# Four residual layers on 8x16x16 images: activations relaid from [sample, w] to [w, sample]

## The chip, the cores and the metric

The kernel runs on one core of one Trainium2 chip. The metric is the device time of one execution in microseconds, as the median of several runs.

## The reference

The input x is fp32, 8192 samples of 8 channels by 16 rows (h) by 16 columns (w). Four layers are applied one after the other, each on a group-normalized copy (4 groups of 2 channels, mean and variance over channel, h and w), with its result added to x:

```python
x = x + tt_matvec([core0, core1, core2], gn(x)) + bias0      # layer 0: tensor-train product, rank 8
x = x + relu(batchnorm(conv3x3(gn(x), w1) + b1))             # layer 1: statistics over all samples
x = x + conv3x3(quant(gn(x)), quant(w2)) / (sx * sw) + b2    # layer 2: sx = 127 / max|gn(x)| over all samples
x = x + conv3x3(edge_pad(gn(x)), sign(w3) * mean|w3|) + b3   # layer 3
```

Layers 1 and 2 each need one number over all samples, so the work falls into three stages.

## The kernel before

The samples are cut into 64 tiles of 128. A tile is a 128x2048 fp32 array: the partition is (channel, h), the free axis is (sample, w), w innermost. The helpers `samples(t)` and `over_w(stat, a, b)` view it as [128, sample, w] and spread a statistic per sample over w. A quarter is 32 samples, 512 columns.

Each engine executes its instructions in the order of the program, which is kept by the wrapper `InOrder`; therefore nearly all instructions carry the line of that wrapper, L43, and are told apart by the names of the tiles. A name before `<-` is the output, those behind it are inputs.

**Stage 1** (layer 0 and the convolution of layer 1) goes quarter by quarter, 256 of them. `limbs`, `fetch` and `expand` split the normalized x and multiply it by core2 (`pu<-core2r,xl`, copied to `u` by ACT). `main` multiplies `u` by the other cores: eight fp32 matmuls of 512 columns into the PSUM tile `po`, each recorded as two. DVE then adds `po` to x (`xs<-po,xs`). `norm_sums` and `norm_stats` (at steps r=1 and r=4 of `main` in each tile's first quarter, for the tile before) sum x and its square over w with `reduce_w` (`s<-xs`, `s<-sq`); `group_stats` finishes them and `norm_apply` writes the padded copy `x1n`. `conv1_scaled` (ACT) and `conv1_input` (POOL) form the inputs `v` of a fast convolution along w, `conv1` multiplies them (`pm`, `pc`), and `conv1_output` (DVE) combines them into `ys`, of which `bn_stats` follows. `po`, `pm` and `pc` come from one PSUM pool with three buffers, one of each per quarter:

```python
pe.matmul(samples(po)[:, a:b], core01[:, r], u[:, a:b, r, :], start=(r == 0), stop=(r == R - 1))
```

**Stage 2** finishes layer 1, takes the group statistics for layer 2 and the largest normalized value. Per tile: load x and y, ReLU with scale and offset (ACT), add (POOL), square (ACT), `sums_pe` (PE, `gs`), a reduction and a transpose on DVE (`s_c`, `psc`), the power on POOL, `to_rows` on DVE (`diag_b`, `rows_c`) and two matmuls (`gb`, `gr`) that spread the statistics, the centring of x (DVE) and the range, a reduction of |x| over w (`top`). The steps of tile i and of the tiles up to three before it alternate. Most tiles are stored (`x2_d`) and 13 stay in SBUF.

**Stage 3** does the convolution of layer 2 and layer 3. The order of its steps is a fixed list: `TURN`, repeated for each tile, with the head `C_HEAD` and the tail `C_TAIL` written out. Per tile: `rows2` and `spread2` give the scale per sample (`ps_a`); `v` multiplies it in and rounds to int8 (DVE); `q` makes bf16 of it (ACT); `c2h0` and `c2h1` are the convolution in two halves (`pq`, six bf16 matmuls each, four of the twelve per tile covering all 512 columns and eight of them 480); `stz` adds the first half to x (DVE); `z1` (ACT) and `add1` (POOL, `bs`) add the second; `sq`, `sums` (`s<-`), `small`, `pow`, `rows3` and `spread3` are the statistics for layer 3 (`ps_r`, `ps_o`); `t` scales (DVE), `hi` (ACT) and `lo` (POOL) split it in two fp32r parts with edge columns; `c` and `corr` add an offset per sample (ACT, POOL); `c3h0` and `c3h1` are the second convolution (`pf`, 24 fp32r matmuls of 512 columns); `out0` and `out1` add it to x (DVE). `pq` and `pf` rotate through two PSUM buffers.

Of the kernel before, what the change touches and what calls it, by code (L numbers as in the profile page):

```python
# [18 lines left out]
P = 128  # L19
# [3 lines left out]
G = 4  # L23
# [24 lines left out]
C_HEAD = """  # L48
rows2:0 spread2:0 v:0 rows2:1 q:0 spread2:1 c2h1:0 rows2:2 bias:0 v:1 spread2:2 rows2:3 c2h0:0 v:2 z1:0 q:1
spread2:3 stz:0 add1:0 bias:1 c2h1:1 sq:0 c2h0:1 z1:1 v:3 sums:0 stz:1 small:0 q:2 add1:1 c2h0:2 c2h1:2 bias:2  # L50
rows2:4 pow:0 sq:1 rows2:5 rows3:0 z1:2 spread2:4 spread3:0 stz:2 t:0 q:3 sums:1 hi:0 c:0 small:1 v:4 add1:2 pow:1
bias:3 c2h0:3 spread2:5 rows3:1 sq:2 c2h1:3 spread3:1 stz:3 lo:0 sums:2 t:1 rows2:6 corr:0 edl:0 small:2 c:1 q:4
z1:3 hi:1 c3h0:0 pow:2 c3h1:0 v:5 add1:3 rows3:2 out0:0 bias:4 out1:0 lo:1 sq:3 q:5 spread3:2 spread2:6 c2h0:4 c:2
corr:1 edl:1 c2h1:4 rows2:7 z1:4 stz:4 t:2 hi:2 sums:3 c3h1:1 small:3 v:6 c3h0:1 out1:1 c2h1:5 pow:3 bias:5 rows3:3
spread3:3 lo:2 out0:1 q:6 spread2:7 rows2:8 z1:5 edl:2 v:7 c:3 add1:4 sq:4 c2h0:5 c3h0:2 bias:6 t:3 corr:2 stz:5
sums:4 c3h1:2 small:4 add1:5 hi:3 out0:2 c2h0:6 pow:4 rows3:4 sq:5 out1:2 spread2:8 stz:6 spread3:4 t:4 lo:3 c2h1:6
z1:6 corr:3 edl:3 sums:5 c:4 hi:4 small:5 pow:5 bias:7 v:8 q:7 add1:6
""".split()
C_TAIL = """
c2h1:-4 sq:-5 rows2:-2 rows3:-6 out1:-8 spread3:-6 rows2:-1 spread2:-2 c2h0:-4 v:-2 sums:-5 stz:-4 z1:-4 q:-3 t:-6  # L60
edl:-7 c3h0:-7 q:-2 small:-5 c2h1:-3 c:-6 out0:-7 c2h0:-2 hi:-6 add1:-4 sq:-4 pow:-5 rows3:-5 z1:-3 spread3:-5
bias:-2 t:-5 stz:-2 lo:-6 edl:-6 sums:-4 small:-4 bias:-3 corr:-6 c:-5 spread2:-1 c2h0:-3 stz:-3 pow:-4 c3h1:-7
hi:-5 out1:-7 c3h0:-6 rows3:-4 spread3:-4 add1:-3 c2h1:-2 sq:-3 lo:-5 z1:-2 out0:-6 v:-1 c3h1:-6 edl:-5 q:-1 add1:-2
sums:-3 t:-4 corr:-5 c:-4 c3h1:-5 out1:-6 small:-3 sq:-2 pow:-3 hi:-4 out1:-5 lo:-4 rows3:-3 bias:-1 sums:-2 c2h1:-1
small:-2 z1:-1 spread3:-3 edl:-4 c2h0:-1 c3h0:-5 c:-3 t:-3 stz:-1 add1:-1 pow:-2 corr:-3 rows3:-2 c3h1:-4 hi:-3
spread3:-2 sq:-1 out0:-5 c:-2 corr:-4 sums:-1 t:-2 lo:-3 hi:-2 small:-1 pow:-1 out1:-4 c3h0:-4 corr:-2 rows3:-1
out0:-4 edl:-3 c3h0:-3 spread3:-1 t:-1 lo:-2 c3h1:-3 out0:-3 edl:-2 out1:-3 hi:-1 c:-1 lo:-1 c3h0:-2 c3h1:-2 edl:-1
out0:-2 c3h0:-1 out1:-2 corr:-1 c3h1:-1 out0:-1 out1:-1
""".split()

# [8 lines left out]
def tile_net(ctx: ExitStack, tc: tile.TileContext, xb, xt_in, pack0, pack1, pack2, out):  # L79
# [84 lines left out]
    def late_constants(late):  # L164
# [99 lines left out]
        mod32 = const.tile([P, 32], F32, name="mod32")  # L264
# [5 lines left out]
        for k, name in enumerate(("sel0", "sel1", "corr")):  # L270

            t = L[name] = const.tile([P, CH], F32, name=name)
            dve.tensor_copy(t.rearrange("p (g n) -> p g n", g=G),
                            mod32[:, G * k:G * k + G].unsqueeze(2).to_broadcast([P, G, CH // G]))
        yield "statistics"

    def diagonal(n):
        ts = []
        for k in range(2):
            t = const.tile([P, NQ, 32], F32, name=f"diag_{n}_{k}")  # L280
            nc.gpsimd.memset(t, 0.0)
            ts.append(t)
        return ts
# [6 lines left out]
    HALVES = [(0, P // 2), (P // 2, P)]  # L290

    def samples(t):
        return t.rearrange("p (b w) -> p b w", w=W)

    def over_w(stat, a, b):

        return stat[:, a:b].unsqueeze(2).to_broadcast([P, b - a, W])

    def reduce_w(dst, src, op=ALU.add):
        for a, b in HALVES:  # L300
            dve.tensor_reduce(dst[:, a:b], samples(src)[:, a:b], AX.X, op)
# [21 lines left out]
    with first as s:  # L323
# [13 lines left out]
        x1n = [const1.tile([P, P, W + 2], F32, name=f"x1n_{k}") for k in range(2)]  # L337
        for t in x1n:
            pool.memset(t[:, :, 0:W + 2:W + 1], 0.0)
# [13 lines left out]
        def add_bias(t):  # L353
            v = samples(T[t]["x"])
            pool.tensor_tensor(v, v, bias0_t.unsqueeze(1).to_broadcast([P, P, W]), ALU.add)
# [76 lines left out]
        def main(t, q, between, n0=None):  # L432
# [3 lines left out]
            for a, b in parts:  # L436
                for r in range(R):
                    for f, args in between.get(r, ()) if b == QS else ():
                        f(*args)
                    pe.matmul(samples(po)[:, a:b], core01[:, r], u[:, a:b, r, :], start=(r == 0), stop=(r == R - 1))  # L440
            cols = slice(q * BANK, (q + 1) * BANK)
            x = T[t]["x"]
            dve.tensor_tensor(x[:, cols], po, x[:, cols], ALU.add)
# [12 lines left out]
        def norm_apply(t):  # L456
            group_spread(spread1, T[t].pop("mv"), 32)
            x, xn = samples(T[t]["x"]), x1n[t % 2][:, :, 1:W + 1]
            for a, b in HALVES:
                for k, op, i in ((0, ALU.subtract, x), (1, ALU.mult, xn)):  # L460
                    dve.tensor_tensor(xn[:, a:b], i[:, a:b], over_w(spread1[:, k], a, b), op)


        def quarter_stats(t, q):
            cols, x = slice(q * BANK, (q + 1) * BANK), T[t]["x"]
            sums = small.tile([P, 2, QS], F32, name=f"sq_{t}_{q}", tag="sums")
            act.activation(xh[:, cols], x[:, cols], AF.Square)
            for k, src in enumerate((x, xh)):
                dve.tensor_reduce(sums[:, k], samples(src)[:, q * QS:(q + 1) * QS], AX.X, ALU.add)
# [3 lines left out]
        def quarter_apply(t, q):  # L473
            spread = spreads[q % 2]
            group_spread(spread, T[t].pop(("mv", q)), 32)
            b = slice(q * QS, (q + 1) * QS)
            x, xn = samples(T[t]["x"])[:, b], x1n[t % 2][:, b, 1:W + 1]
            for k, op, i in ((0, ALU.subtract, x), (1, ALU.mult, xn)):
                dve.tensor_tensor(xn, i, over_w(spread[:, k], 0, QS), op)
# [4 lines left out]
        def conv1_scaled(t, q):  # L484

            x = x1n[t % 2][:, q * QS:(q + 1) * QS]
            x4, x2 = (wk.tile([P, QS, n], F32, name=f"{k}_{t}_{q}", tag=k, bufs=1) for k, n in (("x4", W), ("x2", W // 2)))
            act.activation(x4, x[:, :, 0:W], AF.Copy, scale=4.0)
            act.activation(x2, x[:, :, 1:W:2], AF.Copy, scale=2.0)
            T[t]["x4", q] = x4, x2  # L490

        def conv1_input(t, q):
            x = x1n[t % 2][:, q * QS:(q + 1) * QS]
            x4, x2 = T[t].pop(("x4", q))
            e, r = (wk.tile([P, n, QS, W // 4], F32, name=f"{k}_{t}_{q}", tag=k, bufs=1) for k, n in (("e", 4), ("r", 2)))
            v = wk.tile([P, 6, QS, W // 4], F32, name=f"v_{t}_{q}", tag="v")
            pool.tensor_tensor(e.rearrange("p k b j -> p b j k"), *(t.rearrange("p b (j k) -> p b j k", k=4)
                                                                    for t in (x[:, :, 2:W + 2], x4)), ALU.subtract)
            pool.tensor_tensor(r[:, 0], x2[:, :, 1:W // 2:2], x2[:, :, 0:W // 2:2], ALU.subtract)
            pool.tensor_tensor(r[:, 1], x[:, :, 4:W + 1:4], x[:, :, 2:W:4], ALU.subtract)  # L500
            pool.tensor_tensor(v[:, 0], e[:, 2], e[:, 1], ALU.add)
            pool.tensor_tensor(v[:, 1], e[:, 2], e[:, 1], ALU.subtract)
            pool.tensor_tensor(v[:, 2], r[:, 1], r[:, 0], ALU.add)
            pool.tensor_tensor(v[:, 3], r[:, 1], r[:, 0], ALU.subtract)
            pool.tensor_tensor(v[:, 4:6], e[:, 2:4], e[:, 0:2], ALU.subtract)
            T[t]["v", q] = v.rearrange("p i b j -> p i (b j)")
# [14 lines left out]
        def conv1_direct(t, q):  # L521

            x = x1n[t % 2][:, q * QS:(q + 1) * QS]
            po = ps_m.tile([P, BANK], F32, name=f"pd_{t}_{q}", tag="mm")
            for k in range(3):
                pe.matmul(samples(po), L["band1"][:, k], x[:, :, k:k + W], start=(k == 0), stop=(k == 2))
            act.activation(T[t]["y"][:, q * BANK:(q + 1) * BANK], po, AF.Identity, bias=L["b1"], scale=1.0)
# [5 lines left out]
        def conv1_stats(t, q):  # L533
            dve.bn_stats(T[t]["bst"][:, q], T[t]["y"][:, q * BANK:(q + 1) * BANK])
# [6 lines left out]
        def conv1_output(t, q):  # L541
# [7 lines left out]
            s1, d3, d1, s3 = sd[:, 0], sd[:, 1], pm[:, 1], pm[:, 3]  # L549
            y = T[t]["y"][:, q * BANK:(q + 1) * BANK].rearrange("p (n k) -> p k n", k=4)  # L550
            ends = wk.tile([P, 2, NC], F32, name=f"ends_{t}_{q}", tag="ends", bufs=1)
            dve.tensor_tensor(ends[:, 0], s1, po[:, 0], ALU.add)
            dve.scalar_tensor_tensor(ends[:, 1], d3, 8.0, po[:, 1], ALU.mult, ALU.add)
# [154 lines left out]
    def sums_pe(ps, x, sq):  # L708

        for k, src in ((0, x), (1, sq)):  # L710
            for q in range(NQ):
                pe.matmul(ps[32 * q:32 * q + 32], L["wsum"][:, k], src[:, q * BANK:(q + 1) * BANK],
                          start=(k == 0), stop=(k == 1))


    def put_quarter(ps):
        nc.vector.tensor_copy(ps[:, 0:NQ], L["quarter"])

    def stats_small(mv, st, ps, name):

        s = small.tile([P, 32], F32, name=f"s_{name}", tag="s")
        dve.tensor_reduce(s, samples(ps), AX.X, ALU.add)
        dve.transpose(st, s)
# [399 lines left out]
```

## Time and profile before

| | us |
|---|---|
| median of 3 runs (lowest, highest) | 3833.41 (3831.76, 3834.64) |
| profiled execution, span from first to last instruction | 3831.5 |
| stage 1: first instruction to last product of layer 1's convolution | 0 to about 2620 |
| stage 2: to the end of the largest value | about 2620 to 3063 |
| stage 3: to the end | about 3063 to 3831 |
| stage 3, first output stored, last output stored (issue) | 3105.8, 3826.4 |

For the profiled execution only its span is listed; the three run times lie 0.3 to 3.1 above it. In the table of busy time by stretch a row gives the stretch, its length, and for each engine the busy microseconds with the number of instructions; then the TensorE clock that was granted (1.00 is full), the busy share of the DMA engines and the bytes per time. In the timeline a row gives the start, the length, the engine, the line, the operation, the tiles, the shape, the count and in brackets the idle time before it with what ended it. Matmul records overlap, so their spacing from start to start, and not their length, is what they cost on a full PE.

### The profile page before, as it was taken

Reading aid. Unit: us, or ns where it says so; the run is one execution under the profiler, and the core shown is the slowest. Engines: PE = TensorE matmul, PEld = TensorE weight load, DVE = VectorE, ACT = ScalarE, POOL = GpSimd, SP = SyncE. Lnnn points to the kernel's source line nnn. Section 1 sums busy time; section 2 is a strip of 40 time slices with the busy share of each in tenths; the row PEclk is TensorE's granted clock in tenths of the full one; section 3 lists DMA queues with packets and bytes.
Section 4 is the critical chain, followed back from the end, with each engine's and each line's share of the span. In section 5 each row is a group of like instructions: output and inputs, shape, how many; then the busy total and the mean of one; then the engine's idle time right before and its main releaser. Section 6 shows DMA issues by size and latency. Waiting matters only on the chain. (4 is left out here: it accounts for less than half of the span.)

```text
span 3831.5 us, 52833 instructions
## 1 busy us (share of the span) xinstructions
PE 3606.5 (94%) x16326; PEld 2127.6 (56%) x16326; DVE 3406.9 (89%) x6319; ACT 2513.1 (66%) x2673; POOL 3040.9 (79%) x3101
## 2 busy tenths in 40 slices
PE   8999999999999999999999999997655599999998
PEld 4666666666666666666666666662211155555555
DVE  8988888888888888888888888877998889999997
ACT  5666666666666666666666666665665477777775
POOL 4877778777777787777777877766887779999997
PEclk9999999999999999999999999998776699999999
DMA  5787787888877878788788788757999724444432
GB/s 212 255 268 258 258 266 251 270 253 262 270 256 258 267 250 271 253 262 267 258 261 266 250 271 252 258 187 281 422 425 425 301 110 176 187 185 178 185 145 99
DMA packets 210809, 960.93 MB, mean 251 GB/s; under 512 B 44896, under 2 KB 45152, under 8 KB 110048
## 3 DMA queue, kind: packets, MB, share of 16 engines
q1 hardware_dynamic: 173808, 692.22, 48.7%
q0 software_dynamic: 36288, 264.26, 23.4%
q8 instruction: 131, 2.15, 0.2%
q14 instruction: 150, 1.23, 0.1%
q10 hardware_dynamic: 432, 1.08, 0.1%
HBM read 578.84 MB, written 378.54 MB: 250 GB/s over the span
## 5 line engine op out<-in xcount | busy, mean ns | idle before, releaser
L43 PE MATMUL po<-u,core 128*128 128x512 f32 (+1 forms) x4112 | 1844.7, 591 | 0.0
L43 ACT COPY u<-pu 128x2048 f32<-128x2048 f32 x512 | 956.7, 1868 | 511.9 <-PE pu L43 511.8
L43 PEld LDWEIGHTS po<-u,core 128*128 128x128 f32 x4112 | 744.7, 190 | 737.1 <-issue 736.1
L43 PE MATMUL pu<-core2r,xl 128*128 128x256 f32 x4032 | 678.5, 310 | 4.5 <-ACT u L43 3.6
L43 PEld LDWEIGHTS pu<-core2r,xl 128*128 128x128 f32 x4032 | 527.9, 189 | 127.8 <-issue 123.0
L43 POOL TENSOR_TENSOR bs<-bs,xh 128x512 fp32r<-128x512 f32 (+1 forms) x253 | 325.6, 1287 | 201.0 <-ACT xh L43 200.9
L43 POOL TENSOR_TENSOR v<-e 128x128 f32<-128x128 f32 x750 | 397.9, 542 | 0.0
L43 DVE TENSOR_TENSOR xs<-po,xs 128x512 f32<-128x512 f32 x256 | 177.0, 692 | 217.5 <-PE po L43 217.5
L43 ACT ACTIVATE m<-pm,b 128x128 f32<-128x128 f32 x250 | 92.0, 368 | 395.5 <-PE pm L43 395.5
L43 PEld LDWEIGHTS pm<-v,fast 128*128 128x128 f32 x2000 | 262.5, 191 | 119.7 <-issue 106.2
L43 POOL TENSOR_TENSOR e<-x1n,x 128x512 f32<-128x512 f32 x250 | 306.2, 1225 | 23.9 <-ACT x L43 16.4
L43 DVE TENSOR_TENSOR bs<-bs,stat 128x1024 f32<-128x1024 f32 x252 | 290.8, 1217 | 2.1
L43 POOL TENSOR_TENSOR xs<-xs,w 128x2048 f32<-128x2048 f32 x64 | 291.5, 4554 | 0.6 <-DMA xs<-in_xt 0.6
L43 PE MATMUL pm<-v,fast 128*128 128x128 f32 x2000 | 263.6, 275 | 0.0
L43 ACT ACTIVATE x<-x1n 128x512 f32<-128x512 f32 x500 | 247.1, 545 | 7.6 <-DVE x1n L43 7.6
L43 POOL TENSOR_TENSOR mv<-mv,mhalf 128x4 f32<-128x4 f32 x127 | 130.8, 1030 | 138.1 <-DVE mv L43 138.1
L43 PE MATMUL pf<-hi,sign 128*128 128x512 f32 x768 | 227.7, 434 | 0.5 <-DVE xs L43 0.5
L43 POOL DMA_DIRECT2D xl<-limb_d x252 | 150.0, 595 | 96.9 <-ACT x L43 29.1
L43 PE MATMUL pf<-lo,sign 128*128 128x512 f32 x768 | 219.4, 423 | 0.0
L43 POOL TENSOR_TENSOR v<-r 128x128 f32<-128x128 f32 x500 | 215.9, 448 | 0.0
L43 ACT ACTIVATE sq<-xs 128x2048 f32<-128x2048 f32 x103 | 196.8, 1911 | 4.7 <-POOL xs L43 4.6
L43 PE MATMUL gb<-rows_c,sel 128*128 128x128 f32 x128 | 40.3, 409 | 167.3 <-DVE rows_c L43 167.3
(310 smaller groups left out, 7202.4 us busy)
## 6 DMA issues: line engine op xcount, KB each, us to landing
xl<-limb_d POOLq DMA_DIRECT2D x252, 1024.0 KB, 7.4
x_d<-xs SPq DMA_DIRECT2D x76, 1024.0 KB, 8.4
xs<-in_xt SPq DMA_DIRECT2D x64, 1024.0 KB, 7.5
bs<-in_xb SPq DMA_DIRECT2D x63, 1024.0 KB, 5.7
limb_d<-xh SPq DMA_DIRECT2D x1008, 64.0 KB, 4.3
limb_d<-bs SPq DMA_DIRECT2D x1008, 64.0 KB, 5.2
y_d<-ys SPq DMA_DIRECT2D x60, 1024.0 KB, 8.0
u<-x_d SPq DMA_DIRECT2D x34, 1024.0 KB, 5.9
```

The source lines that it names most:

```text
L43: return self.tc.keep_in_program_order(op(*args, **kwargs))
```

## The change

All tiles get the free axis (w, sample), sample innermost; the host writes the input and reads the output accordingly. `by_w(t)` views a tile as [128, w, sample], a quarter is now 32 samples at each of 16 w (`quarter_of_samples`), and `over_w(stat)` repeats a row of statistics for each w.

In stage 1 `main` reads `u` as before and writes `po` with a step of 32 elements. `reduce_w` reads along w with a step of 128 elements (512 bytes). The other steps keep their operations and take new views:

```diff
-pe.matmul(samples(po)[:, a:b], core01[:, r], u[:, a:b, r, :], start=(r == 0), stop=(r == R - 1))
+pe.matmul(po.rearrange("p (w b) -> p b w", w=W)[:, a:b], core01[:, r], u[:, a:b, r, :], start=(r == 0), stop=(r == R - 1))
 ...
 def reduce_w(dst, src, op=ALU.add):
     for a, b in HALVES:
-        dve.tensor_reduce(dst[:, a:b], samples(src)[:, a:b], AX.X, op)
+        dve.tensor_reduce(dst[:, a:b], by_w(src)[:, :, a:b].rearrange("p w n -> p n w"), AX.X, op)
 ...
-y = T[t]["y"][:, q * BANK:(q + 1) * BANK].rearrange("p (n k) -> p k n", k=4)
+y = by_w(T[t]["y"])[:, :, quarter_of_samples(q)].rearrange("p (j k) b -> p k j b", k=4)
```

In stages 2 and 3 the sums over w are formed by PE: 32 matmuls of 128 columns go into four strips of 32 partitions and are folded by one more product. Statistics are spread by a broadcast on ACT (`wide`) and a product with the identity; the reductions, transposes and `diag` writes on DVE go, and `range2` reads along w with the step of 512 bytes:

```diff
 def sums_pe(ps, x, sq):
     for k, src in ((0, x), (1, sq)):
-        for q in range(NQ):
-            pe.matmul(ps[32 * q:32 * q + 32], L["wsum"][:, k], src[:, q * BANK:(q + 1) * BANK],
-                      start=(k == 0), stop=(k == 1))
+        for w in range(W):
+            rows = slice(32 * (w % 4), 32 * (w % 4) + 32)
+            pe.matmul(ps[rows], L["wsum"][:, k], by_w(src)[:, w], start=(k == 0 and w < 4), stop=(k == 1 and w >= W - 4))
+def fold_pe(st, rows):
+    pe.matmul(st, rows, L["mod32"][:, 0:2 * G], start=True, stop=True)
+def wide(dst, src):
+    act.copy(dst.rearrange("p (g n) -> p g n", n=CH // G), src.unsqueeze(2).to_broadcast([P, src.shape[1], CH // G]))
+def spread_pe(dst, col):
+    pe.matmul(dst, col, ident, start=True, stop=True)
 ...
 for i in range(NT + 4):
     on(i, sum2)
     on(i - 2, sums2)
+    on(i - 3, wide2)
+    on(i - 2, copy2)
     on(i - 3, spread2)
+    on(i - 2, fold2)
     on(i - 1, square2)
     on(i - 2, stats2)
```

In stage 3 both convolutions read and write whole runs of columns. Both halves of layer 2 are added by DVE; `z1`, `add1` and `bias` go, and the bias of layer 2 is taken in by the square, the sums, `t` and `c` instead:

```diff
-for n in range(3):
-    pe.matmul(samples(pc[:, k]), L["sign3"][:, n], tv[:, :, n:n + W], ...)
+for n in range(3):
+    pe.matmul(pc[:, k], L["sign3"][:, n], T[i][t][:, 4 * q + n:4 * q + n + 4].rearrange("p w n -> p (w n)"), ...)
 ...
+def first2(i, h):
+    x = halves(T[i]["x"])[:, h]
+    dve.scalar_tensor_tensor(x, T[i].pop(("pq", h)), inv, x, ALU.mult, ALU.add)
 ...
-    dve.tensor_tensor(samples(t)[:, a:b], samples(x)[:, a:b], over_w(r3, a, b), ALU.mult)
+    dve.scalar_tensor_tensor(by_w(t)[:, a:b], by_w(x)[:, a:b], L["bias2"], over_w(r3, b - a), ALU.add, ALU.mult)
```

Ten of the twelve `pq` matmuls of a tile then have 512 columns and two have 384. `spread3` becomes four steps: `turn3` (rows to columns by a product with the identity), a copy on ACT, and the two products of before. The written lists `TURN`, `C_HEAD` and `C_TAIL` give way to one sorted order, a start time per step and a period:

```diff
+PERIOD = 10.78
+PHASE = {"wide": 0, "spread2": 0.01, "v": 0.02, "q": 11, "c2h0": 13.3, "stz0": 18.2, "c2h1": 19.6, "stz1": 21.4, "sq": 25.8,
+         ...
+         "edl": 76.6, "c3h1": 84.2, "out1": 85.4, "c3h0": 86.3, "out0": 86.31}
 ...
+todo = [(op, i) for _, op, i in sorted((PERIOD * i + at, op, i) for op, at in PHASE.items() for i in range(NT))]
```

## The prediction

> **What bounds the kernel now.** I read the busy rows of the page first, then the table of busy time by stretch, since an average over stages with different limits says little.
>
> ```profile
> span 3831.5 us, 52833 instructions
> PE 3606.5 (94%) x16326; PEld 2127.6 (56%) x16326; DVE 3406.9 (89%) x6319; ACT 2513.1 (66%) x2673; POOL 3040.9 (79%) x3101
> ```
>
> ```profile
> core 0: us, PE busy (x) PEld busy (x) DVE busy (x) ACT busy (x) POOL busy (x), PEclk, DMA share, GB/s
> 100.00:2600.00 2500.00, 2499.80 (x10902) 1550.09 (x10902) 2211.04 (x4280) 1621.50 (x1856) 1922.20 (x2665) 1.00 0.79 257
> 2700.00:2950.00 250.00, 149.75 (x768) 48.22 (x772) 235.40 (x363) 151.94 (x152) 208.48 (x77) 0.73 1.01 425
> 3110.00:3750.00 640.00, 639.95 (x3211) 375.35 (x3210) 596.74 (x1054) 497.51 (x441) 624.56 (x223) 1.00 0.45 175
> ```
>
> The rows are stages 1, 2 and 3. Stage 1 (to about 2620): PE never pauses, DVE has 12% to spare. Stage 2 (to 3063): the DMA engines are full (1.01, 425 GB/s), DVE 94%. Stage 3: PE is full and POOL 98%. A busy PE need not be PE at its peak, so I went to starts in the timeline. First PE and then DVE in the quarter of stage 1 where DVE does the group statistics:
>
> ```profile
> 1522.49 3.60 PE L43 MATMUL po<-u,core 128*128 128x512 f32 x8
> 1525.93 1.05 PE L43 MATMUL pm<-v,fast 128*128 128x128 f32 x8
> 1526.82 0.61 PE L43 MATMUL pc<-v,fast 128*128 128x128 f32 x4
> 1527.18 1.19 PE L43 MATMUL pu<-core2r,xl 128*128 128x256 f32 x8
> 1528.20 1.02 PE L43 MATMUL po<-u,core 128*128 128x512 f32 x2
> ```
>
> ```profile
> 1516.65 2.34 DVE L43 TENSOR_REDUCE s<-xs 128x64 f32<-128x1024 f32 x2
> ...
> 1522.03 2.35 DVE L43 TENSOR_REDUCE s<-sq 128x64 f32<-128x1024 f32 x2 [0.23 <-ACT sq L43]
> ...
> 1526.13 0.69 DVE L43 TENSOR_TENSOR xs<-po,xs 128x512 f32<-128x512 f32 x1 [0.22 <-PE po L43]
> ```
>
> Eight records of the main product take 3.44 us from start to start, 0.43 us each: PE really is full. The reader is to see how little slack DVE has here. The eviction `xs<-po` waited only 0.22 us for PE and one earlier reduction 0.23 us for ACT, where the quarter before it shows a wait of 1.70. Of the three PSUM buffers `mm`, each quarter takes three (po, pm, pc), so the next po (1528.20) needs the one evicted at 1526.13 to 1526.82: 1.38 us of room and no more.
>
> **What the Trainium skill says.** (1) "PSUM — Partial Sum Buffer", Specifications (TRN2): lines of 8 bytes, and a non-contiguous pattern slows matmuls significantly. The trace has one case, bf16 `pq` written in runs of 15 of 16: it starts every 0.216 us with 480 columns, exactly as with 512 contiguous ones (3404.80, 3405.02, 3405.23). A split line seems to cost one full slot, 0.83 ns. (2) "Vector Engine (DVE) Microarchitecture Reference", Measured stream behaviour on trn2: one source hopping at every element takes 1.73 ns per column instead of 1.05. The trace agrees in two small reductions, below. (3) "TensorE: Matmul & The Clock Gate", Part 3: matmuls into different 32-column strips run together. The trace agrees: four `s` matmuls start 7 ns apart and the group takes 0.43 us.
>
> **Stage 1, part by part.** *Main product with a stepped write.* 16 fp32 records per quarter, 512 columns in 0.427 us, 0.83 ns per column. That equals the slot of a single line, so I take a cost of nothing. It holds if the two beats of an fp32 column land in one line. For that speaks that the fp32 product, reading runs of 16, keeps 0.43 us, while the one-beat `pf`, reading runs of 16 in 18, takes 0.26 us where 512 columns of `pq` take 0.216: the fp32 column hides its gaps. Bounds: 0 to a doubling (16 x 0.427 x 256 quarters = 1750 us). A gain is excluded, since nothing is removed.
>
> *Strided reductions.* The sums over w now step 512 B through SBUF. The trace has no such step at this size; two reductions of 128 elements stand in for it.
>
> ```profile
> L43 DVE TENSOR_REDUCE mod<-ident x1: 374/374/374, 87.2 to 87.2; 128x32 f32<-128x128 f32 x1
> ```
>
> ```profile
> L43 DVE TENSOR_REDUCE quarter<-ident x1: 274/274/274, 87.5 to 87.5; 128x4 f32<-128x128 f32 x1
> ```
>
> `mod` steps 128 B, `quarter` is contiguous: 100 ns over 128 elements, 0.78 ns each. `shz`, with 64 B, took 368. I take 0.72 ns, 0.74 us per reduction of 1024; bounds 0 and 1.5 us (the skill's worst row, 2.5 ns). Four per tile lie in that one quarter: 4 x 0.74 = 2.96 us more. Back come 0.24 (the four `ys` writes become contiguous: 1.14 us from the first to bn_stats, which becomes about 0.9 at the spacing 0.20 of the `ends` writes) and the waits of 0.23 and 0.22 plus some 0.05 of queue. The eviction comes 2.96 - 0.24 - 0.50 = 2.2 us late; PE has 1.38 less 0.05 for the signal. **PE stands 0.9 us per tile, 63 tiles: +55 us.** Behind the reductions in DVE's queue stand the output transform and the eviction; PE waits for the eviction, and everything for PE. The other three quarters have 0.8 to 1.7 us of slack and repay DVE's lag, but PE gets nothing back, being full.
>
> The other stage 1 edits are layout alone: same instructions, same element counts, inner runs of 32 or 128; hidden behind PE (ACT 65%, POOL 77%, with room for some 2 us per quarter). Nothing is taken off PE.
>
> **Stage 2.** Off DVE: `diag`, `rows_c`, `s_c`, `psc`, together 1.48 us from start to start (3019.98 to 3021.46). On: two strided range reductions, 2 x 0.74 = 1.48. DVE stays at 6.07 plus a quarter of the 1.4 us of `top` and `amax`, 6.4 us per tile against DMA's 6.58 (250 us, 38 tiles). ACT gets a copy (128) and a broadcast (256), some 0.7 us on 4.0. PE has 64 short records instead of 16, off the path at 60% busy. The new broadcast stands behind `relu` on ACT, which waits for the y load, and DVE's centring now waits for it: a phase shift, with loads some seven tiles ahead. I take +3 us; -5 to +25 (up to +100 at 1.5 us per reduction).
>
> **Stage 3.** The period is 11.55 us (starts of the `pf` block in the chain, 3132.74, 3144.29, ...). By starts: `pf` 24 x 0.26 = 6.24, `pq` 12 x 0.217 = 2.61, sums 1.86, three spreads 0.67: 11.37 on PE. POOL: 4.27 (`lo`) + 3.70 (`c`) + 2.42 (`bs`) + 1.02 (power) = 11.41.
> After, PE: `pf` reads 512 contiguous columns. The contiguous one-pass `pu` takes 0.116 for 256, so 0.22 to 0.232 for 512; I take 0.229, 5.50. `pq`: 10 x 0.216 + 2 x 0.163 = 2.49. Sums: 32 matmuls in strips, 64 records of 128 columns, 16 groups of four by 0.111 (128-column spacing of `pm`) = 1.8; up to 2.6 if issue limits. Four 128-column products 0.89, the fold 0.2 to 0.3. Sum 10.9 to 11.0.
> POOL: `bs` goes, `c` is read contiguously and may rise to the 4.55 of the plain add: 9.8. DVE: v 2.43, four PSUM passes of 1.26 to 1.29, t 2.55, two small ones 0.32: 10.4 by durations, about 10 with overlap; `s_d`, four transposes and the `diag` writes go. ACT: about 8.2. `ps_c` still rotates two buffers among four products, each freed by DVE in the same order. Period 11.0: **64 x 0.55 = -35 us.** Fill and drain, now one sorted order instead of a written one: PE's idle of some 27 us there I leave unchanged, ±10. Range of the stage: -50 to +20.
>
> **Sum.** +55 + 3 - 35 = +23. The profiled span is 3831.5, the median 3833.4, the difference lies around the span and stays: 3856 us.
>
> **Rivals.** *Faster: the delay stays inside the slack.* Place: the eviction in the statistics quarter. The stall is 4p - 2.07 us with p the extra per reduction; it is zero at p = 0.52, and the kernel is faster by over 0.2% (7.7 us, about what a measurement of this kernel can tell from no change) from p below 0.60. For it: p was measured at 128 elements and other steps. Against: two steps agree. Stage 3 then decides: 3833 - 38 = 3795. *PE's gain in stage 3 does not come:* `pf` stays at 0.26 because of its type, 24 x 0.26 lifts PE to 11.7, +10 us instead of -35, or the sums are bound by issue (+50). Against it stands `pu`. With stage 1's loss: 3905. *The stepped write is slow:* some of the 1750 us, up to 5580; PE has nothing to hide it. For it the skill's sentence, against it the 0.43 us above. That the edit leaves PE's load in stage 1 unchanged is part of all but the last.
>
> **How the numbers follow.** Forecast 0.49, stall absorbed 0.34, no gain in stage 3 0.11, slow write 0.06. Faster: 0.31 + 0.02 = 0.33. Same: 0.03 + 0.06 = 0.09. Slower: 0.41 + 0.11 + 0.06 = 0.58. Range: from 3785 (absorbed, good drain) to 3915; outside it lie the slow write and part of the last two. The forecast's own range is 3833 to 3885.
>
> **What would show it.** `po` still 0.43 from start to start; `s<-xs` at 1.95 us and not 1.21; PE with one gap of 0.9 us per tile before po, released by DVE's `xs<-po`, so that stage 1 ends near 2675; stage 2's DVE per tile at 6.4; `pf` at 0.23, `bs` gone from POOL, stage 3 taking 733 us instead of 768. Wrong if `s<-xs` stays under 1.8, or if PE shows no such gap, or if `po` is spaced wider.

## Result and profile after

The changed kernel takes 3960.14 us (median of 4 runs, 3957.82 to 3962.43) where the kernel before takes 3833.88 (4 runs): a ratio of 1.0331, 95% interval 1.0316 to 1.0345, or 126 us slower. The prediction was 3856, with a range from 3785 to 3915.

In the profiled executions the ends of the stages are the start of the last product `pd` of layer 1, the start of the reduction over partitions that ends the largest value (`gm`), and the end of the span. The period of stage 3 is the time from one tile's output to the next.

| | before, us | after, us | change | predicted |
|---|---|---|---|---|
| stage 1 | 2619.3 | 2680.0 | +61 | +55 |
| stage 2 | 444.1 | 450.6 | +6.5 | +3 |
| stage 3 | 768.1 | 828.0 | +60 | -35 |
| span | 3831.5 | 3958.6 | +127 | +23 |

Two stages came out as worked out, the third did not. First the busy rows of the page and the busy time by stretch (columns as before):

```profile
span 3958.6 us, 65657 instructions
PE 3635.9 (92%) x22793; PEld 2384.5 (60%) x22856; DVE 3471.2 (88%) x5481; ACT 2428.6 (61%) x2996; POOL 2940.5 (74%) x3036
```

```profile
100.00:2600.00 2500.00, 2460.07 (x10665) 1520.09 (x10664) 2280.28 (x4178) 1577.12 (x1818) 1855.36 (x2611) 1.00 0.78 254
2750.00:3000.00 250.00, 157.83 (x2633) 136.15 (x2637) 247.08 (x213) 169.44 (x228) 210.17 (x77) 0.72 1.01 423
3250.00:3850.00 600.00, 552.26 (x5254) 400.79 (x5294) 471.80 (x481) 356.80 (x528) 484.77 (x145) 1.00 0.43 166
```

PE, which was full in stages 1 and 3, now stands: 40 us of 2500 in stage 1, and 48 of 600 in stage 3. In stage 3 no other engine is full either (DVE 79%, POOL 81%, ACT 59%). When no engine is full, what bounds the stage is not a sum of work but a chain of waits. Stage 2 still has the DMA engines full, and DVE now 99% busy.

**Stage 1.** The timeline of PE and of DVE, and two rows of the costliest groups:

```profile
1519.86 1.17 PE L43 MATMUL pu<-core2r,xl 128*128 128x256 f32 x8
1521.69 3.70 PE L43 MATMUL po<-u,core 128*128 128x512 f32 x8 [0.66 <-DVE xs L43]
```

```profile
1508.72 0.69 DVE L43 TENSOR_TENSOR xs<-po,xs 128x512 f32<-128x512 f32 x1 [1.92 <-PE po L43]
1509.32 3.87 DVE L43 TENSOR_REDUCE s<-xs 128x64 f32<-128x1024 f32 x2
...
1515.68 3.81 DVE L43 TENSOR_REDUCE s<-sq 128x64 f32<-128x1024 f32 x2
...
1520.95 0.68 DVE L43 TENSOR_TENSOR xs<-po,xs 128x512 f32<-128x512 f32 x1
```

```profile
L43 PE MATMUL po<-u,core 128*128 128x512 f32 (+1 forms) x4112 | 1851.5, 593 | 40.6 <-DVE xs L43 40.6
L43 DVE TENSOR_REDUCE s<-xs 128x64 f32<-128x1024 f32 x126 | 243.9, 1973 | 0.0
```

Two stepped reductions take 3.87 us where two contiguous ones took 2.34. The eviction that they delay has no wait of its own any more, and PE's `po` waits for it. From start to start PE loses more than the 0.66 in brackets, because the ends of its records are modelled: a tile of stage 1 takes 41.24 us instead of 40.33, 0.91 more. The stepped write of `po` costs nothing: its records still start 0.43 us apart.

**Stage 3.** PE, ACT, the waits of the stretch 3250 to 3850 (microseconds in all, how often, the longest), and the chain of work:

```profile
3500.46 1.65 PE L43 MATMUL pf<-hi,sign 128*128 128x512 f32 x6
3501.95 1.57 PE L43 MATMUL pf<-lo,sign 128*128 128x512 f32 x6
3504.46 0.46 PE L43 MATMUL ps_t<-ident,rows 128*128 128x128 f32 x2 [0.94 <-ACT S_d L43]
```

```profile
3502.15 1.91 ACT L43 CAST hi<-xh 128x2048 fp32r<-128x2048 f32 x1 [3.51 <-PE pf L43]
3503.96 0.35 ACT L43 ACTIVATE S_d<-ps_t,sbias 128x128 f32<-128x128 f32 x1
```

```profile
ACT hi L43 <- PE pf L43: 168.4, 48, 3.5
...
PE ps_t L43 <- ACT S_d L43: 45.2, 48, 0.9
```

```profile
3500.70 1.42 PE pf L43 x6
3502.12 0.02 issue
3502.15 1.91 ACT hi L43
3504.05 0.27 ACT S_d L43
3504.32 0.14 issue
3504.46 0.46 PE ps_t L43 x2
```

Read the chain from the bottom. The small product that turns the statistics from rows to columns (`ps_t<-ident,rows`) waits for ACT to copy the sums (`S_d`). It does not use these sums: it writes other columns of `ps_t`, the PSUM bank that holds them. `S_d` stands in ACT's queue behind `hi`. And `hi` waits 3.5 us for the `pf` products that still read its buffer, one of two. So once per tile PE has to finish the six `pf` products that read this buffer, then ACT has to do `hi` and `S_d`, and only then PE goes on. Meanwhile PE has only the six products of `lo` to do: from start to start, 1.1 us are lost (3501.95 + 1.40 for six products is 3503.35; the next one starts at 3504.46). The period is 12.49 us; it was 11.55.

The kernel before had no such loop. In its stretch 3250 to 3750 PE waits for nothing, and `hi` waits for its own input from DVE and not for PE (`sq` and `xh` are the two buffers of this input):

```profile
ACT hi L43 <- DVE sq L43: 50.2, 22, 2.3
```

### The profile page after: what moved, and what is told of

It reads as the page before. It is cut to its first block, busy times and chain, and to the rows that moved or that the text cites. A ratio compares the mean times of both kernels' runs of the same rounds, so it can differ in the third digit from the quotient of the medians.

```text
span 3958.6 us, 65657 instructions
## 1 busy us (share of the span) xinstructions
PE 3635.9 (92%) x22793; PEld 2384.5 (60%) x22856; DVE 3471.2 (88%) x5481; ACT 2428.6 (61%) x2996; POOL 2940.5 (74%) x3036
## 5 line engine op out<-in xcount | busy, mean ns | idle before, releaser
L43 POOL TENSOR_TENSOR e<-x1n,x 128x512 f32<-128x512 f32 x250 | 319.6, 1278 | 19.3 <-ACT x L43 13.3
L43 POOL TENSOR_TENSOR mv<-mv,mhalf 128x4 f32<-128x4 f32 x63 | 65.3, 1037 | 288.8 <-DVE mv L43 183.5
L43 DVE TENSOR_REDUCE s<-xs 128x64 f32<-128x1024 f32 x126 | 243.9, 1973 | 0.0
L43 ACT ACTIVATE x<-x1n 128x512 f32<-128x512 f32 x500 | 234.5, 520 | 9.7 <-DVE x1n L43 9.7
L43 DVE TENSOR_REDUCE s<-sq 128x64 f32<-128x1024 f32 x126 | 240.2, 1950 | 0.0
L43 POOL TENSOR_TENSOR xs<-xs,w 128x2048 f32<-128x2048 f32 x64 | 230.4, 3600 | 0.7 <-DMA xs<-in_xt 0.6
L43 POOL TENSOR_TENSOR mvb<-mvb,mhalf 128x4 f32<-128x4 f32 x64 | 66.3, 1035 | 200.0 <-DVE mvb L43 200.0
L43 PE MATMUL pf<-hi,sign 128*128 128x512 f32 x768 | 211.2, 410 | 1.4 <-DVE u L43 1.4
L43 PE MATMUL pf<-lo,sign 128*128 128x512 f32 x768 | 200.9, 397 | 2.3 <-POOL lo L43 2.3
```

The lines of the kernel that those rows point to most:

```text
L43: return self.tc.keep_in_program_order(op(*args, **kwargs))
```

## Experiments

Theory 1: the loss of stage 1 is the stepped reductions on DVE and nothing else in the new layout. Theory 2: the loss of stage 3 is the loop PE, `hi`, `S_d`, PE, not PE's work. The rival in stage 3 (rival A) is that the two buffers of `hi` set the period by themselves, whatever stands behind.

**Stage 1 with contiguous reductions**, the layout kept:

```diff
-            dve.tensor_reduce(dst[:, a:b], by_w(src)[:, :, a:b].rearrange("p w n -> p n w"), AX.X, op)
+            dve.tensor_reduce(dst[:, a:b], src.rearrange("p (n w) -> p n w", w=W)[:, a:b], AX.X, op)
```

> The changed kernel, with stage 1's four sums over w per tile reading contiguous elements instead of every 512 bytes; they therefore add other elements (the statistics of layer 1's normalization are not the reference's), with the same count of elements. Theory 1 (the stepped reductions make DVE late for the eviction of po, and PE waits): s<-xs back at 1.21 us, no idle time of PE before po, stage 1 ends near 2620 instead of 2680, total near 3900 (-60). Rival (the stepped PSUM write or another edit of the layout costs PE's time): stage 1 still ends near 2680, total near 3960.

Measured 3895.06 us (ratio to before 1.0161, 1.0145 to 1.0176): 65 less than the changed kernel. `s<-xs` takes 1.21 us, stage 1 ends at 2614.5, and PE is full again:

```profile
100.00:2600.00 2500.00, 2499.48 (x10902) 1549.85 (x10901) 2157.92 (x4278) 1606.42 (x1856) 1888.55 (x2660) 1.00 0.80 257
```

With the step gone stage 1 ends 5 us earlier than in the old layout. A tile takes the same 40.33 us in both, so these 5 us lie at the ends of the stage. Theory 1 holds.

**The step alone in the kernel before**, where a contiguous read becomes one with 512 bytes between elements:

```diff
-            dve.tensor_reduce(dst[:, a:b], samples(src)[:, a:b], AX.X, op)
+            dve.tensor_reduce(dst[:, a:b], src.rearrange("p (w n) -> p n w", w=W)[:, a:b], AX.X, op)
```

> The kernel before, with only the four sums over w per tile in stage 1 reading every 512 bytes; they add other elements than the reference's. Nothing else of the change is in it. Theory 1: s<-xs at 1.95 us, PE waits some 1 us per tile before po (the ys writes stay stepped here, so a little more than in the changed kernel), stage 1 ends at 2685 to 2695, stages 2 and 3 as before, total 3895 to 3910. Rival (the loss of stage 1 comes from another edit): total within 10 us of 3834.

Measured 3911.07 (1.0203, 1.0186 to 1.0220), 78 us slower than before and just above what was expected; stage 1 ends at 2698.8 and the period of stage 3 is unchanged. That the old layout loses 79 us in stage 1 and the new one 61 has a place in the rows: the new one saves time on DVE elsewhere. Its `ys` writes take 0.28 us each, those of the old layout 0.38 to 0.40.

**The turned statistics in another bank**: the product of the chain writes `ps_o` instead of `ps_t`.

```diff
-        r2, r3, o3, turned = (t[:, 0:P] for t in (ps_a, ps_r, ps_o, ps_t))
+        r2, r3, o3 = (t[:, 0:P] for t in (ps_a, ps_r, ps_o))
+        turned = ps_o[:, P:2 * P]
```

> The changed kernel, with the PSUM tile 'turned' moved from the bank of s3 (ps_t) to the bank of o3 (ps_o). Theory 2 (the product that turns the rows has to wait for ACT's copy S of the sums because both lie in one bank; S stands behind hi on ACT, and hi waits for PE to finish with its buffer, so PE waits for itself): the wait of 0.94 us per tile on S_d is gone, period of stage 3 at 11.4 to 11.6 us instead of 12.49, total 3900 to 3910. Rival A (the two buffers of hi set the loop, whatever PE does): period stays above 12.2, total above 3945. Rival B (PE's own work has grown): the wait goes, but PE is full at 12.4.

Measured 3911.42 (1.0204, 1.0189 to 1.0219), 49 us less than the changed kernel, period 11.70, slightly over what was expected. PE's wait for `S_d` is gone. The rest is in PE's timeline: the copy `rows`, also behind `hi` in ACT's queue, is now the late one.

```profile
3502.43 0.38 PE L43 MATMUL ps_o<-ident,rows 128*128 128x128 f32 x2
...
3504.63 0.49 PE L43 MATMUL ps_r<-rows,sel 128*128 128x128 f32 x2 [0.23 <-ACT rows L43]
```

`hi` still waits 3.8 us for `pf` in each tile, at a period 0.8 shorter. Rival A falls: that wait costs something only through what stands behind it.

**`hi` later in the order**: its start time in the sorted order moves behind those of `S` (33.2 + 3 x 10.78 = 65.5) and `rows` (56.7 + 10.78 = 67.5).

```diff
-"hi": 65.3
+"hi": 67.6
```

> The changed kernel, with the start time of hi in the order of stage 3 raised from 65.3 to 67.6, so that on ACT the copy S, the edges of lo and the copy of the rows come before hi. Theory 2: S no longer stands behind hi, PE does not wait for it, period 11.4 to 11.6 us, total 3900 to 3915, though both tiles still share the bank. Rival A (the buffers of hi): hi still waits for PE, starts later, period 12.5 or more, total 3960 or more.

Measured 3890.06 (1.0148, 1.0133 to 1.0163): 70 us less, by one number, and 10 below the range that was expected. The period is 11.31 us, no wait of PE is left, and PE is full:

```profile
3250.00:3800.00 550.00, 547.44 (x5325) 410.38 (x5367) 477.50 (x486) 355.31 (x534) 493.54 (x147) 1.00 0.47 181
```

Theory 2 holds: both tiles still share the bank, and with the order alone the loop is gone. What stays open is whether PE has to wait for `S_d` because the two lie in one bank or because they are parts of one tile, `ps_t`; the run before this one moved `turned` out of both. The same run gives PE's own work per tile, by starts: `pf` 5.77 us, `pq` 2.58, sums 1.89, the small products 1.06, together 11.30.

**Both causes taken out.** Besides the later `hi`, half of the sum of x (samples 0 to 63, complete after the second quarter) moves into the last quarter of the same tile, where DVE has slack (`norm_sums_early` calls `reduce_half` for that half).

```diff
-            reduce_w(T[t]["s"][:, 0], T[t]["x"])
+            reduce_half(T[t]["s"][:, 0], T[t]["x"], 1)
...
+            if q == 3 and not last:
+                at(4, True, norm_sums_early, t)
```

> The changed kernel with two edits: hi at 67.6 in the order of stage 3, and in stage 1 the stepped sum over the first 64 samples moved from the statistics quarter to the quarter before, where DVE waits 1.92 us for PE. All four reductions stay stepped and the arithmetic is the reference's. Theories 1 and 2 together: what counts is not the DVE time added but the quarter it falls in, so PE's wait before po disappears, stage 1 ends at 2619 to 2626, stage 3 keeps its period of 11.3 us, total 3826 to 3840. If the stepped reductions cost in another way (their length anywhere, or by disturbing PE's reads), stage 1 stays above 2650 and the total above 3860.

Measured 3835.54 (13 runs; ratio 1.0005, 0.9996 to 1.0013): even with the kernel before. PE is full again in stage 1, although all four stepped reductions are still there:

```profile
100.00:2600.00 2500.00, 2498.10 (x10890) 1550.64 (x10889) 2326.62 (x4269) 1607.36 (x1854) 1885.80 (x2660) 1.00 0.79 257
```

The two causes add up: 125 us less than the changed kernel, 56 in stage 1 (it ends at 2624.4) and 70 in stage 3. Against the kernel before, stage 1 is 5 us longer, stage 2 7 longer and stage 3 9 shorter. The shorter period brings some 62 x 0.24 = 15 us; the first `pf` comes 47.7 us after `gm` instead of 34.5, 13 lost. What is left, about 7 gained, is 10 gained at the end less 3 lost between the first `pf` and the first output: from the ninth-last output to the last it takes 73.4 us, where it took 85.4, and 2 of these 12 are the shorter period.

**The head of stage 3 drawn together**: the start times of the first six tiles are multiplied by 0.55 to 0.93.

```diff
+        early = [0.55, 0.62, 0.7, 0.78, 0.86, 0.93] + [1.0] * NT
-sorted((PERIOD * i + at, op, i) ...
+sorted((PERIOD * i + at * early[i], op, i) ...
```

> As moved_hi, with the start times of the first six tiles in stage 3's order drawn together (times 0.55 to 0.93). If the sorted order loses at the start of stage 3 because DVE scales six tiles before the first t, the first pf comes 8 to 15 us earlier (47 us after the largest value in hi_later, 35 in the kernel before) and the total falls by as much, 3815 to 3830. If PE's own work or the latency of one tile's chain sets the start, it stays within 3 us of moved_hi.

A miss: 3894.24 (1.0157, 1.0143 to 1.0170), 59 us worse than without it. The first `pf` comes 54.7 us after `gm`, the first outputs follow each other by 16 to 25 us instead of 11.3, and the later period is unchanged. PE stands for a small step of another engine:

```profile
3144.36 0.80 PE L43 MATMUL ps_a<-ident,wide_d 128*128 128x128 f32 x2 [7.37 <-ACT wide_d L43]
```

Late steps of an early tile now stand in the queues ahead of the first steps of the next ones: `wide_d` stands in ACT's queue behind `sq`, which waited 5.38 us for DVE's addition of `pq`, and this stands in DVE's queue behind an earlier tile's output `u<-pf`, which waited 1.69 us for PE. What sets the longer start of stage 3 stays open.

**Contiguous range in stage 2**, a single run: the two reductions of |x| read contiguously.

```diff
-by_w(T[i]["x"])[:, :, a:b].rearrange("p w n -> p n w")
+T[i]["x"].rearrange("p (n w) -> p n w", w=W)[:, a:b]
```

> The changed kernel, with stage 2's reductions of the range reading contiguous elements; they take the largest of other sets of elements, so the scale may differ a little from the reference's. Stage 2 took 451 us with the change and 444 before. If DMA sets its pace (full at 423 GB/s), it loses at most some 10 us of the 451 although DVE is freed of 1.5 us per tile; if DVE at 98.8% sets it, stage 2 falls by 50 us or more.

Stage 2 takes 442.8 us instead of 450.6 (450.5 to 451.7 in all other runs with the changed layout). It gains no more, though DVE's load falls from 99% to 75%:

```profile
2750.00:3000.00 250.00, 155.68 (x2590) 133.81 (x2590) 186.78 (x205) 164.10 (x221) 205.06 (x75) 0.71 1.01 423
```

The DMA engines set the pace, and the stepped reductions cost 8 us there.

**Sums by additions of halves.** Three kernels, all with `hi` later, tried to do without the stepped reductions: x is added in halves along w (1024, 512, 256, 128 columns), every operand contiguous. The first does so for both sums.

```diff
+    def tree_w(dst, src, tmp):
+        n = W // 2
+        dve.tensor_tensor(tmp[:, 0:n], src[:, 0:n], src[:, n:2 * n], ALU.add)
+        ...
-            reduce_w(T[t]["s"][:, 0], T[t]["x"])
+            tree_w(T[t]["s"][:, 0], by_w(T[t]["x"]), x1n[t % 2][:, 1:W // 2 + 1])
-            reduce_w(T[t]["s"][:, 1], sqs[1])
+            tree_w(T[t]["s"][:, 1], by_w(sqs[1]), by_w(sqs[1])[:, 0:W // 2])
```

> The changed kernel with hi drawn later (67.6) and, in stage 1, the two sums over w formed by four additions of halves each (1024, 512, 256 and 128 columns, all contiguous) in place of two stepped reductions. From the rows of the changed kernel: 1.22 + 0.69 + 0.42 + 0.28 = 2.6 us per sum instead of 3.9, so the statistics quarter is 0.4 us longer than with contiguous reductions (4 x 1.21 = 4.84 against 5.2), inside the slack of 0.5. The theory that the stepped reductions alone cost stage 1 its time: no wait of PE on xs, stage 1 ends at 2614 to 2622, the rest as with hi later alone: 3820 to 3835 us, which is even with the kernel before or up to 0.35% faster. Rival: the additions use the tile of the normalized copy as scratch; if its readers of two tiles before are still at work, DVE waits for POOL or ACT there, the eviction comes late again and stage 1 ends beyond 2640, 3850 or more.

A miss: 3937.11 (1.0272, 1.0258 to 1.0286), 47 us worse than `hi` later alone; stage 1 ends at 2726.3. The timelines of DVE and of POOL:

```profile
1498.04 4.04 DVE L43 TENSOR_TENSOR x1n<-xs 128x1024 f32<-128x1024 f32 x1
1502.12 1.15 DVE L43 TENSOR_TENSOR x1n<-x1n 128x512 f32<-128x512 f32 x2
```

```profile
1497.78 0.46 POOL L43 TENSOR_TENSOR r<-x 128x128 f32<-128x128 f32 x1
...
1500.28 0.71 POOL L43 TENSOR_TENSOR v<-e 128x256 f32<-128x256 f32 x1
1503.85 1.27 POOL L43 TENSOR_TENSOR bs<-bs,xh 128x512 fp32r<-128x512 f32 x1 [2.85 <-ACT xh L43]
```

The addition shows no wait, yet it takes 4.04 us; it ends at 1502.08, 1.1 us after POOL's run of instructions ends at 1500.99, and 1.2 us is all that an addition of this size takes elsewhere. Both its operands lie in SBUF; the operations of the changed kernel on 1024 columns in this stage, at 1.2 us, have one operand in PSUM or only one operand. The next run moves this sum behind the output transform of the quarter (`norm_sums` at r = 1 keeps only the square; `tree_w` of x goes to r = 4), where POOL has done.

> The kernel with the additions by halves, with the first sum moved behind the output transform of the same quarter (r = 4 instead of r = 1), so that it starts when POOL has finished forming v. In the run before this one the first addition, which reads two SBUF tiles, took 3.99 us instead of 1.22: it ended 1.1 us after the last of a run of eight POOL instructions began to leave the engine free, in every tile but the first. Theory: DVE stood there for POOL; out of POOL's run it takes 1.2 us, at most one POOL instruction of 1.27 (lo of the split) falls beside the additions, the eviction of the quarter comes within PE's room, stage 1 ends at 2614 to 2630 and the time is 3820 to 3840. Rival: the additions are slow for another reason (the tile x1n, its readers, the square on ACT); then the first one stays near 4 us and the time stays at 3925 to 3945.

3879.52 (1.0119, 1.0102 to 1.0136), stage 1 ends at 2667.3. Outside POOL's run the first addition takes 1.22 us, so its mechanism holds; it writes the same scratch tile `x1n` as before, so the rival of the first of these runs, the readers of that tile, falls. The time was missed. A group of DVE's additions beside POOL's next instruction shows why in part:

```profile
L43 DVE TENSOR_TENSOR x1n<-xs 128x1024 f32<-128x1024 f32 x49 | 59.6, 1216 | 0.0
L43 DVE TENSOR_TENSOR sq<-sq 128x1024 f32<-128x1024 f32 x49 | 111.3, 2271 | 0.0
```

The first addition of the squares, whose operands both lie in SBUF too, now falls on POOL's subtraction of 1.33 us. The third kernel keeps the stepped reductions for the squares alone.

```diff
-            tree_w(T[t]["s"][:, 1], by_w(sqs[1]), by_w(sqs[1])[:, 0:W // 2])
+            reduce_w(T[t]["s"][:, 1], sqs[1])
```

> As the run before this one, but only the sum of x is formed by additions of halves (at r = 4, behind the output transform); the sum of squares keeps its two stepped reductions of 1.95 us, which read one SBUF tile. In the run before, the first addition of x took 1.22 us, but that of the squares 2.27, since POOL's subtraction of the split (1.33 us) fell beside it, and stage 1 ended at 2667. Here DVE has 2.6 + 3.9 us instead of 4 x 1.21 = 4.84: 1.7 more, less 0.24 for the contiguous writes and 0.5 of slack, so the eviction is 1.0 us late against a room of 1.33. Theory (one SBUF operand: no standing for POOL; the eviction inside the room): no wait of PE on xs, stage 1 ends at 2614 to 2626, 3820 to 3838 us. Rival: any lateness costs, with no room (PE has none, being full): 0.9 us a tile as before, stage 1 near 2680, 3885 to 3895.

3876.49 (1.0114, 1.0097 to 1.0131), stage 1 ends at 2664.3: a miss again. DVE's timeline shows what was left out:

```profile
1502.37 0.42 DVE L43 TENSOR_TENSOR sd<-m,pm 128x256 f32<-128x256 f32 x1 [0.76 <-ACT m L43]
```

The sum that was moved had covered the wait of the output transform for ACT's `m`. In its new place it leaves DVE idle for 0.76 us (0.75 in the run before this one; with `hi` later alone DVE does not wait there). The eviction comes 1.81 us late instead of 1.0, nearly all of the difference being this gap, and a tile takes 40.90 us, 0.57 more than PE needs. No run tested this account further. None of these kernels is faster than the one before; the best is the one with both causes taken out, which is even with it.

## Why the prediction was wrong

**Stage 1: right in size and cause.** The stepped reductions take 1.97 and 1.95 us (predicted 1.95). The eviction came 12.23 us after the one before it instead of 10.08, 2.15 late (predicted 2.2), and PE lost 0.91 us per tile (0.9). The end at 2680 was given as near 2675. The step of the PSUM write was costed at nothing, and is; the reason given, that both beats of a column land in one line, no run tested. The rival that the delay stays inside the slack falls with p = 0.75, where it needed 0.52.

**Stage 2: right.** +6.5 where +3 (-5 to +25) was given. DVE is 99% busy, some 6.5 us per tile where 6.4 on 6.58 was worked out; removing the steps returned 8 us, in the one run of it.

**Stage 3: the step that failed is "Period 11.0: 64 x 0.55 = -35 us".** It was wrong twice.

- *The missing wait* is the larger part, 70 us of the 95 between -35 and +60. The step set the period equal to PE's sum. It looked for PSUM buffers only at `ps_c` and noted that these rotate as before. It did not follow the new `turn3` to the bank that it shares with the sums, the copy of the sums to its place in ACT's queue, or the `hi` ahead of it to the buffer that waits for `pf`. All three could be read in the changed kernel: `ps_t` holding both `turned` and `s3`, the start times 65.3 and 65.5, and `hi` among the tiles with two buffers. "PSUM — Partial Sum Buffer" of the Trainium skill, in the section on bank collisions, says that the compiler's back end orders any two instructions on different engines that touch the same bank and quadrant, reads and writes alike. The trace agrees in so far as PE's write waited 0.94 us for ACT's read of other columns; it does not show what put the two in order.
- *PE's sum was mis-sized.* It is 11.30 and not 10.9 to 11.0. `pf` takes 5.77 against 5.50: within a run the spacing is 0.233 (0.229 was taken), and the first of each twelve takes about 0.32. `pq` takes 2.58 against 2.49, the sums 1.89 against 1.8, and the small products 1.06 against 1.1 to 1.2. The prediction's own sum for the kernel before, 11.37, was short in the same way: PE was full there, at a period of 11.55, and the first `pf` of a tile took 0.37 us where 0.26 was counted. Setting a sum that leaves this out against a measured period makes the gain too large: it is 15 us and not 35.
- *The head* was left unchanged at ±10. Without the wait, the first `pf` is 13 us later than before.

Together these make 70 + 20 + 13 = 103 us of the 95 that were missed; the 7 or so gained near the end stand against it.

The rival "PE's gain in stage 3 does not come" had the right sign for the stage (+10, or +50 with the sums bound by issue, where +60 came), but by another mechanism, so that its nearness is luck: `pf` did get faster (0.233) and the sums were not bound by issue (1.89). The rival of the slow stepped write falls. Two sums of the rivals are off, without effect on the outcome: the absorbed delay leaves +3 - 35, which is 3801 and not 3795, and +55 + 3 + 10 is 3901 and not 3905.

The confirmed signs were the wrong ones to stop at. `po` at 0.43, `s<-xs` at 1.95, the gap before `po`, `pf` at 0.23 and `bs` gone from POOL all came true, and none of them tests whether PE stays full in stage 3. The one that does, 733 us for the stage, failed at 828.

## What to carry to other kernels

When an order of steps is rewritten, the sum of work of the fullest engine is only a lower bound of the period: take every new small step, name the bank and the buffer that it shares, the instruction ahead of it in its queue, and what that one waits for. If a small step stands behind a large one that waits for the engine it must feed, put it ahead; here one start time was worth 70 us. And before a delayed instruction is moved, ask what wait it covers where it stands.

## What the runs showed of the hardware that was not expected

- The fp32 product writes PSUM with a step of 128 bytes at the pace of the contiguous write: 0.43 us for 512 columns in both kernels. The prediction had counted on it, against the sentence on non-contiguous patterns that it takes from the Trainium skill; for this product the measurement decides.
- A DVE addition with both operands in SBUF stood for the rest of POOL's run, 2.9 us over seven instructions, and not for one alone. "SBUF — State Buffer" of the Trainium skill, "SBUF: two separate sides", says that a DVE operation with two SBUF inputs and a GpSimd operation lock each other out for a whole instruction. The runs agree on the lock (1.22 us outside the run, 3.99 within it), but DVE did not get its turn between POOL's instructions. The profile shows this as a long instruction and not as a wait.
- POOL adds a 128x2048 tile in 3.60 us when one operand repeats along the inner axis (`xs<-xs,w` after), and in 4.55 when it doesn't (`xs<-xs,w` before). In stage 3 the change goes the other way, 3.70 before and 4.59 after (`xs<-xs,c`), as the prediction had allowed.
